# Layer 0 of a four-layer graph-attention stack: centring the norm by ScalarE's bias in place of a VectorE subtraction

## The chip, the cores and the metric

The kernel runs on one core of one Trainium2 chip. The metric is the device time of one execution in microseconds (us). Profiles are of one execution; their span goes from the first to the last instruction.

## The reference, cut to what matters

The input `x` is 8 batches x 2048 nodes x 64 features, and `adj` is a sparse 2048 x 2048 adjacency. Four layers follow one another. Each has the form `x = x + attention(relu(layernorm(x)), adj)`, where the norm is taken over the 64 features of each batch and node, without weights:

```python
def _layernorm(x, axis=-1, eps=1e-5):
    m = jnp.mean(x, axis=axis, keepdims=True)
    v = jnp.var(x, axis=axis, keepdims=True)
    return (x - m) / jnp.sqrt(v + eps)
```

Layer 0 is masked dot-product attention, softmax(h h^T / 8) h over the edges. Layer 1 is additive attention (GAT) with an ELU, layer 2 a four-head dot-product GAT with an output norm, layer 3 additive attention with a ReLU. What matters here is the norm that layer 1 takes of the `x` that layer 0 leaves: mean, variance, `(x - m) * rstd`, ReLU. The kernel computes it at the end of layer 0.

## The kernel before, in words

**Tiles.** All eight batches of a node lie in one row of 8 x 64 = 512 columns (`F`), so that a tile is 128 nodes x 512 columns, and there are 16 tiles (`NT`). The kernel works on edges, not on the dense matrix: each tile has lists of neighbours, a few of one neighbour per row (`ROWS`) and a few of packed edges (`PACKED`), and for each it gathers 128 rows of a table in HBM by an indirect DMA (`gather`, line 259). The table holds the normed `x` of all nodes (`store_rows`, line 363), with a row of column means as its last but one (lines 366 to 375: GpSimd sums the rows in `acc`, TensorE adds over the partitions, and a DMA writes the row). So the first gather of a layer needs all 16 tiles of the layer before.

**Stages.** `pipeline(*stages)` (line 218) goes over the tiles in a given order and runs stage s of tile n - s at step n, the oldest tile first. Two pipelines make up the time up to the end of layer 0. The first (line 710) loads `x`, norms it (`norm_a`, `norm_b`, `scaled`) and stores table 0. The second (line 711) has nine stages: load the adjacency tile; build the neighbour lists (`lists`, VectorE work for the most part); gather (`take0`); scores and exponentials (`first0`, with the load of the tile's `x`); row sums and the weighted sum of the gathered rows (`second`, whose products of rows and weights, line 389, run on GpSimd in layer 0, and whose sums run on TensorE); `third0`; `pre_b`; `pre_c`; `pre_d`. Layer 1 (line 719) ends in the same last stages.

**The norm.** `third0` divides by the row sums (line 480) and calls `add_store`: x is added (line 488), stored (line 489) and handed to `norm_a`. This has two forms. With `centre`, VectorE sums each batch (276), makes the mean in a small piece of a PSUM bank (`tiny`, 280) and subtracts it from the tile (283, into `ln_xc`), and ScalarE squares the centred tile in one instruction of 512 columns (284). Without `centre`, VectorE writes the negative mean to SBUF (`ln_m`, 288), and ScalarE squares x in eight instructions of 64 columns, one per batch, each with that batch's negative mean as bias (290). `norm_b` sums the squares (296), scales them (297), and GpSimd takes the power -1/2 (299); where the mean was not taken off, GpSimd also multiplies negative mean and rstd (301). `scaled` (307) applies rstd, and in the second form that product as bias, in eight ScalarE instructions of 64 columns together with the ReLU. Then TensorE transposes (315), ScalarE copies (316), two small products for layer 1's attention follow (354 to 357), and the rows are stored.

The first norm of layer 0, and the one after layer 1, take the form without `centre`; the norm after layer 0 and the two of layer 2 take the form with it.

**Buffers.** `x` tiles come from a pool of six buffers (line 498), `ln_xc` from one of three (282), `ln_m` from one of four. A buffer is free again when its last reader is done.

**What sets the order.** Every engine works through its own queue in order. The order in each queue is set when the program is built, by a list scheduler that simulates the engines and takes, of what is ready, what comes first in the program. So the order of the trace is not that of the source, and is fixed at run time: an instruction whose input is late holds all that stand behind it on its engine. Loads and stores issued by `nc.sync` stand in SP's queue, gathers in GpSimd's.

Of the kernel before, what the change touches and what calls it, by code (L numbers as in the profile page):

```python
# [61 lines left out]
def edge_stack(ctx: ExitStack, tc: tile.TileContext, x_in, adj, w1, w1t, a1, wh, wht, bh, wo, bo,  # L62
# [210 lines left out]
    def norm_a(src, st, centre):  # L273

        s = small.tile([P, B], F32, name="ln_s")
        nc.vector.tensor_reduce(s, heads(src), AX.X, OP.add)
        st["sq"] = rows_pool[0].tile([P, F], F32, name="ln_sq", bufs=4)
        if centre:
            mean = tiny(B)
            nc.vector.tensor_scalar(mean, s, INV_D, None, op0=OP.mult)  # L280
            st["less"] = None
            st["src"] = rows_pool[0].tile([P, F], F32, name="ln_xc", bufs=3)
            nc.vector.tensor_tensor(heads(st["src"]), heads(src), wide(mean), op=OP.subtract)
            nc.scalar.activation(st["sq"], st["src"], AF.Square)
            return
        st["src"] = src
        st["less"] = small.tile([P, B], F32, name="ln_m")
        nc.vector.tensor_scalar(st["less"], s, -INV_D, None, op0=OP.mult)
        for b in range(B):
            nc.scalar.activation(st["sq"][:, b * D:(b + 1) * D], src[:, b * D:(b + 1) * D], AF.Square,  # L290
                                 bias=st["less"][:, b:b + 1])
# [187 lines left out]
    def divide(st, dst):  # L479
        nc.vector.tensor_tensor(heads(dst), heads(st["y"]), wide(st["rec"]), op=OP.mult)  # L480

    def third0(i, st):
        divide(st, st["y"])
        add_store(i, st, st["y"], True)

    def add_store(i, st, p, centre, more=0.0):
        x = st["x"]
        nc.vector.scalar_tensor_tensor(x, p, more, x, op0=OP.add, op1=OP.add)
        nc.sync.dma_start(out=xs[i], in_=x)
        norm_a(x, st, centre)  # L490
# [98 lines left out]
    with tc.tile_pool(name="rows", bufs=2) as rp:  # L589
        rows_pool[0] = rp  # L590
        sel_all[0] = rp.tile([P, sum(PACKED) * P], F32, name="sel", bufs=1)
        with tc.tile_pool(name="lists", bufs=2) as pool, \
# [28 lines left out]
            def lists(i, st):  # L621
# [69 lines left out]
                for t0 in range(0, T, step):  # L691
# [7 lines left out]
                    for t in range(n):  # L699
# [9 lines left out]

            pipeline(xin_rows, lambda i, st: norm_a(st["x"], st, False), pre_b, pre_c(None), pre_d(0, None))  # L710
            pipeline(load_adj, lists, take0, both(first0, xin_rows), second, third0, pre_b, pre_c(u1),
                     pre_d(1, u1))

# [738 lines left out]
```

## Time and profile before

| | |
|---|---|
| Median of 3 runs | 1661.34 us (1655.29 to 1661.87) |
| The profiled execution | 1662.6 us, its span 1660.9 us |
| PE (TensorE matmul) busy | 1214.6 us, 73% |
| DVE (VectorE) busy | 1311.9 us, 79% |
| ACT (ScalarE) busy | 741.6 us, 45% |
| POOL (GpSimd) busy | 1151.1 us, 69% |
| First L488 of layer 0 (x added) | 153.5 us |
| Last scaling (L307) of layer 0 ends | 396.95 us |
| First gather of layer 1 starts | 404.64 us |
| Layer 0's stage, 150 to 390 us: DVE, POOL, PE, ACT busy | 232.0, 179.4, 168.3, 87.1 of 240 us |

A line of the trace names the source line (L283 is line 283), the engine, the operation, its output and inputs by the program's names, and their shapes. "POOL" is GpSimd, "PEld" TensorE's weight load, "SPq" SP's DMA queue; a "q" after an engine's name is its sequencer. In a timeline each row gives start, length, engine, line and operation; several equal instructions in a row are merged ("x8"), and in brackets stands how long the engine had been idle and what released it. In the view of a source line the three numbers are the minimum, median and maximum length in ns of one instruction.

### The profile page before, as it was taken

To read this page: it belongs to the slowest core of one execution; us is meant where nothing else is said; L and a number is where in the kernel's file an instruction comes from. 1 tells how busy PE (TensorE), PEld (TensorE's weight loads), DVE (VectorE), ACT (ScalarE), POOL (GpSimd) and SP (SyncE) were. 2 spreads that over 40 slices of the span, in tenths; PEclk is the share of its full clock that TensorE was granted. 3 is DMA by queue.
4 is the path that set the end of the run, shared out by engine and by line. 5 is a ranking of instruction groups with operands and counts; after the bars stand their busy time and mean duration, and the time that the engine had idled before them with its cause. 6 is when DMAs were issued, how large, how long until landed. Compare 5 with 4: busy or idle time off the path is not lost. (4 is left out here: it accounts for less than half of the span.)

```text
span 1660.9 us, 15702 instructions
## 1 busy us (share of the span) xinstructions
PE 1214.6 (73%) x3771; PEld 606.7 (37%) x3771; DVE 1311.9 (79%) x2674; ACT 741.6 (45%) x2362; POOL 1151.1 (69%) x903
## 2 busy tenths in 40 slices
PE   0025576776789974599997999999576868846898
PEld 0012243343454541234343344443233424423555
DVE  5978999994669987799999799861179979954667
ACT  5851223443257783356632455554334445560011
POOL 5765866786764215899689889998277889656650
PEclk9998877986889997799999999999877978857899
DMA  5545554453776537656255345300273443126771
GB/s 167 181 163 179 171 191 164 140 193 125 213 256 231 183 157 271 233 180 222 92 202 184 123 142 188 138 13 13 102 259 121 146 127 114 64 77 198 228 213 63
DMA packets 85787, 266.94 MB, mean 161 GB/s; under 512 B 14627, under 2 KB 14659, under 8 KB 75446
## 3 DMA queue, kind: packets, MB, share of 16 engines
q0 software_dynamic: 37328, 141.05, 27.4%
q1 hardware_dynamic: 48358, 124.79, 21.0%
q8 instruction: 32, 0.52, 0.1%
q14 instruction: 69, 0.57, 0.1%
HBM read 208.74 MB, written 57.05 MB: 160 GB/s over the span
## 5 line engine op out<-in xcount | busy, mean ns | idle before, releaser
L259 POOL DMA_INDIRECT g<-table,idx x405 | 396.2, 978 | 222.4 <-issue 131.7
L782 POOL TENSOR_TENSOR wh<-g,w 128x1024 f32<-128x1024 f32 x162 | 307.3, 1917 | 30.0 <-PE y L797 27.9
L394 PE MATMUL y<-wg,ident 128*128 128x512 f32 x392 | 232.4, 720 | 74.4 <-POOL wg L389 67.8
L299 POOL TENSOR_TENSOR ln_r<-ln_q,mhalf 128x8 f32<-128x8 f32 x80 | 135.9, 1702 | 129.0 <-DVE ln_q L297 93.0
L769 DVE TENSOR_REDUCE s<-prod 128x32 f32<-128x2048 f32 x81 | 183.9, 2285 | 14.6 <-ACT w L771 14.4
L389 POOL TENSOR_TENSOR wg<-g,w 128x1024 f32<-128x1024 f32 (+1 forms) x91 | 160.0, 1767 | 39.7 <-ACT w L445 31.7
L797 PE MATMUL y<-wh,ident 128*128 128x512 f32 x320 | 154.3, 609 | 28.1 <-POOL wh L795 24.4
L394 PE MATMUL y<-wg,selt 128*128 128x512 f32 x256 | 142.7, 669 | 6.0 <-POOL wg L389 6.0
L394 PEld LDWEIGHTS y<-wg,ident 128*128 128x128 f32 x392 | 79.6, 223 | 160.4 <-POOL wg L389 82.8
L797 PE MATMUL y<-wh,selt 128*128 128x512 f32 x256 | 124.6, 613 | 10.4 <-POOL wh L782 10.4
L805 ACT ACTIVATE yn<-y,rec 128x64 f32<-128x64 f32 x512 | 110.7, 366 | 27.6 <-PE y L797 26.8
L765 DVE TENSOR_TENSOR prod<-q,g 128x2048 f32<-128x2048 f32 x49 | 111.4, 2274 | 5.2 <-ACT g L763 5.1
L389 DVE TENSOR_TENSOR wg<-g,tiny 128x1024 f32<-128x1024 f32 (+1 forms) x92 | 98.1, 1086 | 12.3 <-PE y L394 11.9
L451 DVE SCALAR_TENSOR_TENSOR zt<-m,bhc,att 128x512 f32<-128x512 f32 x64 | 47.2, 737 | 74.9 <-ACT att L450 74.8
L408 PE MATMUL m<-w,selt 128*128 128x8 f32 (+1 forms) x384 | 61.0, 262 | 54.0 <-ACT w L554 19.1
L408 PEld LDWEIGHTS m<-w,selt 128*128 128x128 f32 x384 | 63.7, 215 | 100.0 <-ACT w L554 26.6
L307 ACT ACTIVATE xh<-x,ln_r 128x64 f32<-128x64 f32 x256 | 88.2, 427 | 25.5 <-POOL ln_r L301 25.4
L797 PEld LDWEIGHTS y<-wh,ident 128*128 128x128 f32 x320 | 58.9, 193 | 104.1 <-issue 64.4
L763 ACT COPY g<-g 128x512 f32<-128x512 f32 x81 | 50.4, 622 | 98.6 <-DVE prod L765 92.6
L437 PE MATMUL q<-rows,sel 128*128 128x512 f32 x128 | 81.4, 739 | 15.4 <-DVE prod L431 8.0
L765 DVE TENSOR_TENSOR prod<-qe,g 128x2048 f32<-128x2048 f32 x32 | 73.0, 2281 | 15.6 <-DMA qe<-qtab,qidx 14.5
L315 PE MATMUL q<-ident,xh 128*128 128x128 f32 x192 | 51.3, 341 | 44.9 <-ACT xh L307 43.1
(208 smaller groups left out, 2593.9 us busy)
## 6 DMA issues: line engine op xcount, KB each, us to landing
qtab<-q SPq DMA_DIRECT2D x16, 1040.0 KB, 4.0
a<-in_adj_dram SPq DMA_DIRECT2D x16, 1024.0 KB, 7.2
q<-qtab SPq DMA_DIRECT2D x14, 1040.0 KB, 5.3
table<-xh SPq DMA_DIRECT2D x48, 256.0 KB, 2.0
rows<-table SPq DMA_DIRECT2D x48, 256.0 KB, 3.8
xs<-x SPq DMA_DIRECT2D x48, 256.0 KB, 2.1
x<-xs SPq DMA_DIRECT2D x48, 256.0 KB, 3.6
table<-xh SPq DMA_DIRECT2D x32, 260.0 KB, 2.4
```

Source lines behind the costliest of these rows:

```text
L259: g = nc.gpsimd.indirect_dma_start(out=ring[:, (held[i] + t) % RING, :cols], out_offset=None, in_=table[k][:, :], in_offset=bass.IndirectO ...
L299: nc.gpsimd.tensor_tensor(st["rstd"][:, 0, :], q, mhalf, op=OP.pow)
L307: nc.scalar.activation(dst[:, b * D:(b + 1) * D], st["src"][:, b * D:(b + 1) * D], func, bias=0.0 if st["less"] is None else r[:, 1, b:b + ...
L389: eng.tensor_tensor(wg[:, :m].rearrange("p t (b d) -> p t b d", b=B), g[:, :, :F].rearrange("p t (b d) -> p t b d", b=B), w[:, t0:t0 + m, ...
L394: nc.tensor.matmul(y, lhs(i, t), wg[:, t - t0, :], start=(t == 0 and own is None), stop=(t == n - 1))
L408: nc.tensor.matmul(p[:, :cols], selt(i, t), packed[:, t, :], start=(t == 0), stop=(t == T - 1))
L437: nc.tensor.matmul(qe, sel(i, t - K), q, start=True, stop=True)
L765: nc.vector.tensor_tensor(pr.rearrange("p (b h) d -> p b h d", h=H), q[:, :B * H * D].rearrange("p (b h d) -> p b h d", h=H, d=D), heads(g ...
L769: nc.vector.tensor_reduce(s[:, t - lo, :], pr, AX.X, OP.add)
L782: nc.gpsimd.tensor_tensor(wg, heads(row(i, t))[:, :, None, :].to_broadcast([P, B, 2, D]), w[:, :, 2 * k:2 * k + 2, None].to_broadcast([P, ...
L797: nc.tensor.matmul(st["ys"][j], lhs(i, t), wg[:, 4 * j:4 * j + 4], start=False, stop=(t == n - 1))
L805: nc.scalar.activation(yn[:, b, h, :], st["ys"][j][:, b, h, :], AF.Copy, scale=st["rec"][:, 4 * j + b, 2 * k + h:2 * k + h + 1])
```

## The change

In `third0`, which only layer 0 uses, the norm is called without `centre`:

```diff
     def third0(i, st):
         divide(st, st["y"])
-        add_store(i, st, st["y"], True)
+        add_store(i, st, st["y"], False)
```

For each of the 16 tiles of layer 0 this has these effects in the program. On VectorE lines 280 (mean to PSUM) and 283 (subtraction, 128 x 512) fall away and line 288 (negative mean to SBUF, 128 x 8) comes in. On ScalarE one Square of 512 columns (284) becomes eight of 64 with a bias (290), and the eight scalings (307) read `x` and not `ln_xc`, and get a bias from SBUF in place of the constant 0. On GpSimd one product of 128 x 8 (301) is added. `ln_xc` isn't used in this layer, and `x` has a later last reader, line 307. No DMA is added, removed or changed. The result is the same up to rounding.

## Prediction

> **What bounds the kernel now.** First, the busy time of each engine by stretch. Columns: stretch, its length, then PE, PEld, DVE, ACT and POOL busy with instruction counts, the granted clock, the DMA share and GB/s.
>
> ```profile
> core 0: us, PE busy (x) PEld busy (x) DVE busy (x) ACT busy (x) POOL busy (x), PEclk, DMA share, GB/s
> 40.00:80.00 40.00, 0.00 (x0) 0.00 (x0) 38.25 (x155) 33.74 (x118) 26.39 (x23) 1.00 0.56 187
> 150.00:350.00 200.00, 135.84 (x418) 71.28 (x418) 193.69 (x577) 66.49 (x229) 143.57 (x105) 0.83 0.48 154
> 350.00:384.00 34.00, 28.87 (x120) 17.11 (x119) 33.24 (x90) 17.06 (x62) 31.77 (x24) 0.95 0.60 208
> 384.00:405.00 21.00, 14.28 (x45) 8.26 (x43) 6.63 (x15) 9.45 (x36) 9.14 (x8) 0.64 0.30 103
> ```
>
> The 16 changed steps lie between 153 us (first L488 of layer 0) and 397 us. Three limits follow one another. From 150 to 350 VectorE is busy 97% and ScalarE 33%: VectorE bounds. From 350 to 384 VectorE (98%) and GpSimd (93%) are both full. From 384 to 405 nothing is full: this is the drain of the last tiles, up to the first gather of layer 1, which needs every row of the table.
>
> Next, the instructions concerned, from the views of their source lines (ns min/median/max). The two of the 8-wide form run in layers 0 (first norm) and 1, with the code that the change switches to.
>
> ```profile
> L280 DVE TENSOR_SCALAR tiny<-ln_s x16: 143/155/170, 159.3 to 388.8; 128x8 f32<-128x8 f32 x16
> L283 DVE TENSOR_TENSOR ln_xc<-x,tiny x16: 625/675/687, 160.5 to 389.0; 128x512 f32<-128x512 f32 x16
> L284 ACT ACTIVATE ln_sq<-ln_xc x48: 613/629/643, 161.3 to 1487.4; 128x512 f32<-128x512 f32 x48
> L290 ACT ACTIVATE ln_sq<-x,ln_m x256: 331/333/351, 19.6 to 625.3; 128x64 f32<-128x64 f32 x128
> L307 ACT ACTIVATE xh<-x,ln_r x256: 423/425/444, 28.4 to 632.7; 128x64 f32<-128x64 f32 x128
> L307 ACT ACTIVATE xh<-ln_xc,ln_r x256: 331/333/361, 174.6 to 1492.8; 128x64 f32<-128x64 f32 x128
> L297 DVE TENSOR_SCALAR ln_q<-ln_q x15: 148/164/2566, 163.5 to 387.2; 128x8 f32<-128x8 f32 x15
> ```
>
> The maximum of L297 is to be seen: 2.57 us for eight columns. The timelines of VectorE and of GpSimd explain such cases; the clearest is L707:
>
> ```profile
> 176.60 3.93 DVE L707 TENSOR_SCALAR idx<-ke 128x2 int32<-128x2 f32 x1
> ```
> ```profile
> 176.19 1.89 POOL L389 TENSOR_TENSOR wg<-g,w 128x1024 f32<-128x1024 f32 x1
> 178.04 0.60 POOL L366 COPY acc<-xh 128x512 f32<-128x512 f32 x1
> 178.61 1.89 POOL L389 TENSOR_TENSOR wg<-g,w 128x1024 f32<-128x1024 f32 x1
> ```
>
> It ends at 180.53, and GpSimd's run of three instructions ends at 180.50. L297 at 201.64 ends at 204.21, an L389 of GpSimd at 204.16. So a small VectorE instruction that reads and writes SBUF is held until GpSimd is through. L280, which writes to PSUM, never exceeds 0.170.
>
> Last, the drain in the timeline:
>
> ```profile
> 387.12 3.81 ACT L307 ACTIVATE xh<-ln_xc,ln_r 128x64 f32<-128x64 f32 x15 [1.18 <-POOL ln_r L299]
> 391.56 0.62 ACT L284 ACTIVATE ln_sq<-ln_xc 128x512 f32<-128x512 f32 x1
> 394.93 2.02 ACT L307 ACTIVATE xh<-ln_xc,ln_r 128x64 f32<-128x64 f32 x8 [0.66 <-POOL ln_r L299]
> ```
> ```profile
> 404.64 1.04 POOL L259 DMA_INDIRECT g<-table,idx  x1 [6.29 <-DMA table<-mr]
> ```
>
> ScalarE works in order: the last tile's Square (input ready at 389.71) starts at 391.56, behind the scaling of the tiles ahead of it.
>
> [...] the trace has 333 and 425, and eight in a row take 2.02 us (pitch 0.241) and 2.76 us (pitch 0.333, at 486.20)[...]. L283 has one input in PSUM, and its spread of 625 to 687 shows no hold.
>
> **The change part by part**, per tile, 16 tiles.
>
> VectorE loses L283. What it frees is the time to the next start: 345.87 to 346.47, so 0.60 us, 9.6 in all. The group's busy time of 10.7 is the other bound.
>
> VectorE loses L280 and gets L288. Unheld they cost the same (0.155; L288 0.162 median in layer 1). But L288 writes SBUF, so it can be held. Layer 1 doesn't show it (maximum 0.172 there), since GpSimd makes no weighted products in it. The like instructions from 150 to 390 do: L297, L652, L654, L707 and L708 sum to 6.7+6.9+6.0+8.6+2.9 = 31.1 us for 60, mean 0.518, which is 0.36 over the 0.16 of an unheld one. Cross-check: L389 fills 76.6 of these 240 us; an arrival at random meets it in 32% of cases and waits half of 1.88, 0.30, and some more for L368. I take 0.36 (16 tiles: 5.8); the bounds are 0 (all as in layer 1) and 0.53 (all as L652).
>
> ScalarE: one Square of 0.54 pitch (0.63 less the overlap) becomes eight in 1.92 (8 x 0.241), and eight scalings of 1.93 become 2.66 (8 x 0.333): 2.1 us more, 34 in all, so 87.1 of 240 us becomes 121, 50%. This lies beside VectorE's work, and costs only where VectorE waits for ScalarE. Its waits now: L412 for L445 2.3, L296 for the Square 0.7. In proportion to the load these grow by 1.2; I take +1. Bounds: 0, and +4. In the 40 us from 40 to 80, with these very 8-wide forms, ScalarE is busy 84% and VectorE still 96%. If the cover goes, each tile pays up to a burst: the slower rival below. Queued behind a burst on ScalarE are L678 (for L679), L428 (for L431), L445 (for GpSimd's L389) and L685.
>
> GpSimd gets L301, 0.202 us in layer 1, 3.2 us in all; hidden until 350 (143.6 of 200 us busy), on the path for the three tiles from 350 to 384: +0.6. Bounds 0 and 3.2.
>
> DMA: nothing is issued, removed or moved. But the scaling now reads x itself, so x's buffer is held from L283 until the scaling, two stages longer, and the next x load behind it on SP's queue is issued later. The pool has six buffers, and the load that goes out at 161.24, after the first L283, serves a tile six ahead, some 90 us later at 15 us per tile. The first scaling ends at 176.7. Cost nothing; if that cover is gone, one landing, 2.9 us.
>
> The drain. Call the last three tiles A, B, C, on the clock of before, with GpSimd's last product ending at 384.06. Square(A) starts at 382.7 (its L288 is held behind one L389), Square(B) at 384.7 to 386.7. Reduction, L297, power (1.65) and L301 (0.2) follow: A is ready at 387.5, B at 389.5. Scaling A 387.5 to 390.2. L480 of C, behind B's reduction, starts at 387.4 instead of 386.65, so C's Square is ready at 389.6. If it goes ahead of scaling B, 390.2 to 392.1, C's power ends at 394.9 and its scaling at 397.8: +0.8 against 396.95. If it goes behind B and B's copy, 393.4 to 395.4, C's scaling ends at 401.0: +4.1. Before has the latter order, so I take +4.1, and keep 0.8.
>
> **Sum.** The first 11 L283s lie before 350 us; the other five lie where GpSimd's block or the drain sets the end, so only 11 count: -11 x 0.60 = -6.6; holds 11 x 0.36 = +4.0; waits for ScalarE +1.0; GpSimd +0.6; drain +4.1. Together +3.1 us. Against the profiled execution (1662.6: span 1660.9 and 1.7 around it) that is 1665.7. That execution is 1.3 over the median of the runs, 1661.3, so the forecast is **1664**. After 405 us everything is only shifted.
>
> **The rivals.** Half a percent, 8.3 us, is about what a measurement of this kernel can tell from no change.
>
> Faster: VectorE's cut passes in full. L288 falls between GpSimd's products, GpSimd's block starts and moves earlier, and C's Square slips ahead: -9.6 + 0.8 = -8.8, about 1652.5. For it: VectorE is full from 150 to 390. Against it: 31 us of held small instructions in that stage, and GpSimd's own 93% from 350.
>
> Slower: ScalarE's bursts stop VectorE. One mechanism: an instruction that VectorE needs, L678 for the selection matrix or L428 for the queries, stands behind a burst of 1.9 or 2.7 us, and VectorE, in order, waits with L679 or L431. One such wait per tile of half a burst, 1.15, in all 16 tiles is 18.4; in half of them 9.2. With +2.1 from the rest, about 1673 to 1682. It decides from (8.3 - 2.1) / 16 = 0.4 us per tile. For it: VectorE's waits for ScalarE are small only because ScalarE is 36% busy. Against it: 40 to 80 us.
>
> That the change does nothing on the chip is ruled out: its lines differ.
>
> **How the numbers follow.** Forecast within half a percent: 0.58. Faster rival: 0.16. Slower rival: 0.22. The forecast's dear corner (holds at 0.53, waits +4) with a drain that is worse than drawn: 0.04, slower. So faster 0.16, same 0.58, slower 0.26. The likeliest case's own range is 1655 (holds 0, drain +0.8, waits 0: -6.6 + 0.6 + 0.8 = -5.2) to 1669 (-6.6 + 5.8 + 4 + 0.6 + 4.1 = +7.9). For 8 in 10 it reaches into both rivals: **1652 to 1673**.
>
> **What would show it.** L283 in layer 0 gone from VectorE and 256 more short activations: certain. L288 between 150 and 400: a mean near 0.5 and single ones over 1 us confirm the hold; all under 0.2 refute it. VectorE's waits for L678, L428 and Square under 5 us in sum confirm the cover; 10 or more mean the slower rival. The first gather of layer 1 at 408 (404.64 + 3.1) tells the sum; the time from GpSimd's last product of layer 0 to that gather, 20.6 now, should be some 24. I am wrong if that gather comes before 398 or after 412, or if later layers change in length by more than a few us.

## The result, and the profile after

| | before | after |
|---|---|---|
| Median of 4 runs | 1661.2 us (1655.29 to 1661.87) | 1701.68 us (1697.76 to 1709.05) |
| The profiled execution, its span | 1662.6, 1660.9 us | 1699.15, 1697.4 us |

The ratio is 1.0248 [1.0224, 1.0273]: the kernel is 2.5% slower, where the prediction had 1664 us and at most 1673. Before any line of detail, the span is cut at the starts of six instructions that both traces have: the first sum of the changed norm (first L276 of `third0`), the first gather of layer 1, the last store of layer 1's query table (L345), the last L846 product of layer 2, the DMA of the row of means ahead of layer 3's gathers (last L375), the last output (L917). All are in us; only the second column holds changed code.

| | up to first sum | sum to gather | layer 1 | layer 2 | up to the mean row | rest |
|---|---|---|---|---|---|---|
| before | 156.1 | 248.5 | 241.8 | 541.7 | 311.6 | 156.6 |
| after | 154.3 | 255.2 | 257.5 | 543.5 | 320.5 | 161.8 |
| difference | -1.8 | +6.6 | +15.7 | +1.8 | +8.9 | +5.2 |

Of the 36.3 us, 31.5 lie in layers 1 to 3, whose source is the same to the letter. How far one profile can be trusted is shown by a second one of before (e9 below): the same stretch of the same program differs in it by up to 3 us.

First the changed part. The view of the engines' busy time by stretch, of the kernel after (the last stretch ends at its first gather):

```profile
40.00:80.00 40.00, 0.00 (x0) 0.00 (x0) 37.71 (x152) 33.46 (x117) 26.39 (x22) 1.00 0.54 182
150.00:350.00 200.00, 138.14 (x422) 72.96 (x420) 190.33 (x580) 89.22 (x312) 148.85 (x120) 0.78 0.51 159
350.00:384.00 34.00, 26.62 (x97) 15.33 (x97) 29.89 (x68) 18.49 (x67) 26.93 (x21) 0.90 0.45 154
384.00:409.00 25.00, 16.81 (x58) 10.08 (x56) 7.93 (x17) 16.13 (x59) 11.38 (x11) 0.66 0.35 119
```

VectorE (the third busy column) falls from 193.7 to 190.3 and from 33.2 to 29.9 us, and ScalarE (the fourth) rises from 66.5 to 89.2 in the long stretch. VectorE is no longer full from 350 to 384. The source-line view of the new step, for all three norms that have it:

```profile
L288 DVE TENSOR_SCALAR ln_m<-ln_s x48: 147/170/1903, 18.1 to 641.4; 128x8 f32<-128x8 f32 x48
```

The maximum of 1903 ns shows the hold; the 16 of layer 0 average 0.53 us (16 rows of VectorE's timeline, added up). The longest runs from 315.02 to 316.92, an L389 of GpSimd from 315.00 to 316.90. The drain, in ScalarE's and GpSimd's timelines:

```profile
390.09 2.76 ACT L307 ACTIVATE xh<-x,ln_r 128x64 f32<-128x64 f32 x8 [0.94 <-POOL ln_r L301]
392.75 2.00 ACT L290 ACTIVATE ln_sq<-x,ln_m 128x64 f32<-128x64 f32 x8
394.66 0.76 ACT L307 ACTIVATE xh<-x,ln_r 128x64 f32<-128x64 f32 x2
```
```profile
409.44 1.04 POOL L259 DMA_INDIRECT g<-table,idx  x1 [7.38 <-issue]
```

The last tile's Squares stand between the scalings of two tiles, and the gather starts 4.8 us later than before.

Now the unchanged part. One wait of VectorE and the longest of GpSimd from 420 us to 680 us, which is layer 1 and the start of layer 2, as the view of waits gives them (total, times, longest), before and then after:

```profile
DVE ln_q L296 <- ACT ln_sq L290: 4.3, 3, 2.0
POOL ln_r L299 <- DVE ln_q L297: 35.4, 5, 8.9
```
```profile
DVE ln_q L296 <- ACT ln_sq L290: 12.3, 8, 2.2
POOL ln_r L299 <- DVE ln_q L297: 71.3, 9, 14.2
```

VectorE waits for the Squares 8 times in place of 3, in a layer that had the eight Squares all along. A likely reason is in the queues, where an instruction that waits stops what stands behind it. In layer 0 of the kernel after, VectorE is idle for 3.15 us until the adjacency load for L626 has landed; L433, the next in its queue, reads what L431 had written by 213.00, and starts at 218.71:

```profile
212.32 0.68 DVE L431 TENSOR_TENSOR prod<-q,g 128x512 f32<-128x512 f32 x1
216.50 2.29 DVE L626 SCALAR_TENSOR_TENSOR a<-a,keyrow 128x2048 f32<-128x2048 int32 x1 [3.15 <-DMA a<-in_adj_dram]
218.71 0.68 DVE L433 TENSOR_REDUCE s<-prod 128x8 f32<-128x512 f32 x1
```

When the rows of both traces are laid side by side, 153 of the 368 rows that VectorE has in layer 1 stand in the same sequence, 178 of the 493 between layer 2 and the row of means, and 769 of ScalarE's 831 in layer 2; behind the row of means all rows of VectorE, ScalarE and GpSimd do. So the list scheduler, which orders all queues when the program is built, dealt other orders to most of what comes behind the change, and the last +5.2 us need another reason.

### The profile page after: what moved, and what is told of

Same layout as the page of the kernel before. It is cut to its first block, busy times and chain, and to the rows that moved or that the text cites. A ratio compares the mean times of both kernels' runs of the same rounds, so it can differ in the third digit from the quotient of the medians.

```text
span 1697.4 us, 15806 instructions
## 1 busy us (share of the span) xinstructions
PE 1227.2 (72%) x3771; PEld 613.8 (36%) x3771; DVE 1316.9 (78%) x2658; ACT 772.5 (46%) x2474; POOL 1156.3 (68%) x919
## 5 line engine op out<-in xcount | busy, mean ns | idle before, releaser
L782 POOL TENSOR_TENSOR wh<-g,w 128x1024 f32<-128x1024 f32 x162 | 307.1, 1917 | 29.6 <-PE y L797 27.5
L299 POOL TENSOR_TENSOR ln_r<-ln_q,mhalf 128x8 f32<-128x8 f32 x80 | 135.7, 1699 | 161.5 <-DVE ln_q L297 138.1
L389 POOL TENSOR_TENSOR wg<-g,w 128x1024 f32<-128x1024 f32 (+1 forms) x91 | 160.3, 1772 | 33.8 <-ACT w L445 17.3
L307 ACT ACTIVATE xh<-x,ln_r 128x64 f32<-128x64 f32 x384 | 133.3, 428 | 42.1 <-POOL ln_r L301 39.3
L805 ACT ACTIVATE yn<-y,rec 128x64 f32<-128x64 f32 x512 | 110.8, 366 | 30.9 <-PE y L797 30.2
L389 DVE TENSOR_TENSOR wg<-g,tiny 128x1024 f32<-128x1024 f32 (+1 forms) x92 | 98.3, 1088 | 18.0 <-PE y L394 17.6
L290 ACT ACTIVATE ln_sq<-x,ln_m 128x64 f32<-128x64 f32 x384 | 96.2, 335 | 34.0 <-DVE ln_m L288 34.0
L437 PE MATMUL q<-rows,sel 128*128 128x512 f32 x128 | 82.7, 747 | 14.8 <-DVE prod L439 9.9
L368 POOL TENSOR_TENSOR acc<-acc,xh 128x512 f32<-128x512 f32 x45 | 61.8, 1373 | 37.0 <-ACT xh L307 36.1
```

Source lines behind the costliest of these rows:

```text
L299: nc.gpsimd.tensor_tensor(st["rstd"][:, 0, :], q, mhalf, op=OP.pow)
L307: nc.scalar.activation(dst[:, b * D:(b + 1) * D], st["src"][:, b * D:(b + 1) * D], func, bias=0.0 if st["less"] is None else r[:, 1, b:b + ...
L389: eng.tensor_tensor(wg[:, :m].rearrange("p t (b d) -> p t b d", b=B), g[:, :, :F].rearrange("p t (b d) -> p t b d", b=B), w[:, t0:t0 + m, ...
L782: nc.gpsimd.tensor_tensor(wg, heads(row(i, t))[:, :, None, :].to_broadcast([P, B, 2, D]), w[:, :, 2 * k:2 * k + 2, None].to_broadcast([P, ...
L805: nc.scalar.activation(yn[:, b, h, :], st["ys"][j][:, b, h, :], AF.Copy, scale=st["rec"][:, 4 * j + b, 2 * k + h:2 * k + h + 1])
```

## Experiments

**Theories.** "Order": layers 1 to 3 are slower because their queues hold another order. Rival "state": they are slower because layer 0 leaves the engines or DMA queues otherwise at run time. For what layer 0 costs there are four: holds of VectorE, ScalarE's bursts, the longer hold of `x`, and layer 0's own order.

**How an order is held.** The built program of one kernel gives, per engine, the sequence of its instructions. This edit adds, in the other kernel, an ordering dependence without a semaphore between each instruction and the next of that list, so that it adds no wait at run time:

```diff
-            order[:] = ORDER1
+            order[:] = ORDER1; mark = len(nc.cur_bb.bb.instructions)
...
+        pin(tc, nc.cur_bb.bb.instructions[mark:])
...
+            if last is not None:
+                tc.add_manual_dep(traced[at], traced[last].name, mybir.DependencyInfo(
+                    mybir.DependencyClass.NoSync, mybir.DependencyReason.DATA), reason="order")
```

From `mark` on it holds layers 1 to 3; without `mark`, layer 0 too. That the hold does this can be read from the traces: in e1 and e10 all rows of VectorE and ScalarE in layers 1 to 3 stand as in before, and in e2 as in the kernel after. That it costs nothing is shown by e17 and e18 (1.0011 and 0.9996), which are held throughout.

The runs were made in five sets. In two of these before itself takes 1705 to 1708 us (e5 to e8; e17 and e18), in the others 1662 to 1664. So ratios are against before in the same set, and stretches are compared among like sets. The last two columns are from the profiled execution, which is one run and can lie some us beside the median.

| run | ratio | sum to gather | layers 1 to 3 |
|---|---|---|---|
| before; again (e9) | 1; 1.0008 [0.9991, 1.0025] | 248.5; 246.7 | 1251.7; 1254.5 |
| after | 1.0248 [1.0224, 1.0273] | 255.2 | 1283.3 |
| e1, change, later order of before | 1.0110 [1.0085, 1.0135] | 254.3 | 1256.5 |
| e10, the same again | 1.0097 [1.0079, 1.0115] | 257.3 | 1251.4 |
| e2, before, later order of change | 1.0166 [1.0138, 1.0193] | 247.0 | 1277.5 |
| e3, change, 8 buffers for x | 1.0119 [1.0085, 1.0154] | 263.9 | 1258.6 |
| e4, before, 7 buffers | 1.0154 [1.0124, 1.0184] | 255.4 | 1271.3 |
| e11, Squares alone, later order held | 1.0108 [1.0088, 1.0128] | 261.5 | 1251.7 |
| e12, biased scaling alone, later order held | 1.0113 [1.0093, 1.0133] | 262.9 | 1258.0 |
| e13, change, 8 buffers, later order held | 1.0063 [1.0043, 1.0082] | 260.2 | 1254.1 |
| e14, change, mean on ScalarE, later order held | 1.0054 [1.0036, 1.0071] | 261.3 | 1250.9 |
| e15, both | 1.0067 [1.0041, 1.0092] | 258.6 | 1252.8 |
| e16, before, 7 buffers, later order held | 1.0081 [1.0061, 1.0102] | 256.2 | 1256.5 |
| e17, before, 7 buffers, all held | 1.0011 [0.9994, 1.0028] | 246.6 | 1296.8 |
| e18, the same but SyncE in layer 0 | 0.9996 [0.9982, 1.0011] | 248.6 | 1301.8 |
| e5, change, all held but SyncE in layer 0 | 1.0089 [1.0068, 1.0111] | 260.5 | 1296.7 |
| e6, the same, mean on ScalarE | 1.0089 [1.0068, 1.0110] | 258.6 | 1302.5 |
| e7, change, 7 buffers | 1.0225 [1.0194, 1.0256] | 262.2 | 1321.4 |
| e8, biased scaling alone | 1.0244 [1.0218, 1.0269] | 262.0 | 1322.7 |

### e1 and e2: the orders of layers 1 to 3 exchanged

e1 is the change with layers 1 to 3 held in the sequences of before, e2 is before with those of the change.

> The changed layer 0, with the instructions of layers 1 to 3 held, on each engine, in the order in which they stand in the kernel before. Theory 'order': of the 36.5 us that the changed kernel's profile shows more, only the 4.8 up to the first gather of layer 1 belong to the changed instructions, and 31.7 to the other order in which the scheduler dealt the unchanged later layers. So about 1661 + 5 = 1666 us (1662 to 1670), and the first gather of layer 1 at about 409. Rival 'state': what layer 0 leaves behind at run time (x buffers freed later, a later start of loads, the granted clock) slows the later layers, whatever their order. So about 1695 to 1702.

> The kernel before, with the instructions of layers 1 to 3 held, on each engine, in the order in which they stand in the changed kernel. Theory 'order': 1661 + 32 = 1693 us (1688 to 1698), with the first gather of layer 1 still at about 405. Rival 'state': about 1661 to 1665.

Measured: 1681.15 us (1675.16 to 1682.5) and 1689.99 us (1686.98 to 1693.52), before there 1663.6. e2 met the number of the order theory. e1 missed both: layers 1 to 3 are back to 1256.5 us, but 1.1% stays. The state theory, which had e1 at 1695 to 1702 and e2 at 1661 to 1665, falls. That the order makes the later layers slower is shown from both sides: before, with not one instruction changed, takes 1277.5 us for them with the other order, 23 to 26 us more than in its own two profiles, and has the same waits in layer 1 as the kernel after. In e2:

```profile
DVE ln_q L296 <- ACT ln_sq L290: 13.1, 8, 2.2
POOL ln_r L299 <- DVE ln_q L297: 71.0, 9, 14.2
```

and in e1 they are near those of before:

```profile
DVE ln_q L296 <- ACT ln_sq L290: 6.3, 4, 2.0
POOL ln_r L299 <- DVE ln_q L297: 27.7, 4, 8.9
```

The same in the busy time by stretch, 500 to 600 us, which lies in layer 1: before, after, e2, e1 in this sequence.

```profile
500.00:600.00 100.00, 92.53 (x341) 48.65 (x339) 95.82 (x187) 77.81 (x214) 30.32 (x32) 0.98 0.54 193
```
```profile
500.00:600.00 100.00, 85.97 (x305) 45.11 (x305) 86.52 (x166) 67.06 (x185) 27.26 (x29) 0.96 0.53 188
```
```profile
500.00:600.00 100.00, 84.29 (x305) 43.95 (x304) 85.19 (x161) 68.93 (x194) 23.97 (x26) 0.98 0.50 177
```
```profile
500.00:600.00 100.00, 94.36 (x351) 49.31 (x349) 95.31 (x190) 73.83 (x201) 30.75 (x33) 1.00 0.60 211
```

VectorE is 96 and 95% busy with the order of before, 87 and 85% with that of the change, whichever work layer 0 has done.

### e3, e4 and e7: only the number of x buffers

e3 and e7 are the change with 8 and 7 buffers for `x`, e4 is before with 7:

```diff
-            load(st, "x", src(i), 6)
+            load(st, "x", src(i), 7)
```

> The change with eight buffers for x in place of six. Here the scheduler's order of layer 1 comes out all but that of before (370 of 372 rows of VectorE the same), that of the layer 2 and 3 norms in between (338 of 493). Theory 'order': layer 1 as long as before (257 us from its first gather to the first load of layer 2's queries, where the changed kernel has 273), part of the rest given back, so 1668 to 1685. Rival 'buffers' (x held two stages longer makes loads late): also layer 1 as before, but then it is the loads, which the waits for x would show. If neither: 1700.

> The kernel before with seven buffers for x: no instruction is added or removed, but the scheduler deals the order of all layers anew (229 of 372 rows of VectorE the same in layer 1, 210 of 493 in the part after layer 2). Theory 'order': the order of before is better than what the scheduler usually deals, so this is slower too, by 10 to 40 us (1670 to 1700). Rival 'state': no change, 1657 to 1665.

> The change with seven buffers for x. The scheduler's order of layer 2 comes out as in the kernel before, that of the part after it nearly so (464 of 493 rows of VectorE), that of layer 1 new. Theory 'order': the part after layer 2 as long as before (some 312 us from the end of layer 2 to the mean row, where the change has 320), layer 1 as it falls (242 to 258 us), so 1667 to 1690. Rival 'state': as the change, 1695 to 1702.

Measured: 1681.23 (1678.32 to 1687.88), 1687.3 (1684.29 to 1689.14) and 1743.77 us (1739.16 to 1749.41; before there 1705.16). e4 does the same work as before with a buffer more, and is 1.5% slower: its layer 1 takes 248.1 and its part up to the mean row 318.2 us. The change is 1.2% slower than before with 8 buffers and 2.25% with 7: buffers act here as a new deal of the queues. No single one of these can be read as the price of a buffer. e3 and e4 fell into the ranges of the order theory. e7 did not: 1667 to 1690 us against a before of 1661 is a ratio of 1.003 to 1.017, and its layer 1, dealt anew, took 277.5 us, where before with every queue held takes 259.0 in such a set (e17).

### e5 and e6: all queues held

e5 is the change with every common instruction of every layer in the sequence of before, except SyncE's in layer 0; L288 stands where L280 stood, the eight Squares where the one did, and L301 behind L299. e6 also makes layer 0's negative mean on ScalarE, so that nothing small is left on VectorE to be held:

```diff
-        nc.vector.tensor_scalar(st["less"], s, -INV_D, None, op0=OP.mult)
+        nc.scalar.activation(st["less"], s, AF.Copy, scale=-INV_D) if early[0] else nc.vector.tensor_scalar(st["less"], s, -INV_D, None, op0=OP.mult)
```

> The change, with every instruction that it shares with the kernel before held in the order of before on VectorE, ScalarE, GpSimd and TensorE in all layers (and on SP from layer 1 on); line 288 stands where 280 stood, the eight Squares where the one stood, 301 behind its 299. What is left is the changed instructions alone. Theory 'order': the time of these is what the prediction's sum gave, near +3 us, with ScalarE's longer steps meeting an order made for short ones (+0 to +7), so 1664 to 1672. Rival 'the change itself': the +17 of the run before, whose layer 0 the scheduler had dealt, is the price of the instructions, so 1676 to 1684.

> As the run with all pinned, but the negative mean of layer 0 (128 x 8) is made by ScalarE, directly ahead of its Squares, and not by VectorE's line 288, which GpSimd can hold. Theory 'hold': line 288 took 0.525 us in the mean in the change, 0.36 over an unheld one, so VectorE's stage is shorter by up to 16 x 0.45 = 7 us, of which some 11 of 16 tiles count: 4 to 5 us less than the run with all pinned. Rival: the hold is hidden, no difference (within 2 us).

Measured: 1720.67 (1715.77 to 1722.68) and 1721.38 us (1715.86 to 1726.83), before there 1705.16: 0.9% each, some 15 us. My theory (0 to 7 us) missed, and the rival (15 to 23 us) holds: in before's own order the change's work costs 15 us. e6 shows that taking L288's holds off VectorE doesn't help: 16 x 0.48 us leave it, for 16 short instructions more on ScalarE, and nothing is gained.

### e8: half of the change, order free

The subtraction and the one Square stay; only the scaling reads `x` with a bias (`i0` is set in layer 0 alone):

```diff
-            st["less"] = None
+            st["less"] = None if i0[0] is None else small.tile([P, B], F32, name="ln_m")
...
-            nc.scalar.activation(st["sq"], st["src"], AF.Square)
+            nc.scalar.activation(st["sq"], st["src"], AF.Square); i0[0] is None or (nc.vector.tensor_scalar(st["less"], s, -INV_D, None, op0=OP.mult), st.__setitem__("src", src))
```

> Half of the change: VectorE still subtracts the mean and ScalarE squares the centred tile in one instruction, but the scaling reads x with a bias, so that 288 and 301 come in and x is held longer. The order from layer 2 on comes out exactly as in the change, that of layer 1 is a third one. Theory 'order': from layer 2's end on as long as in the change and in the run of before with the order of the change (320 us to the mean row), and slower in all by 10 to 40 us: 1672 to 1700. Rival 'Squares' (the eight short Squares on ScalarE make the loss): little loss here, 1662 to 1670.

Measured: 1747.65 us (1744.37 to 1748.86), 2.4%. From layer 2 on it has the very order of the change, and costs as much, without having taken anything off VectorE or added a Square. The rival, which made the Squares the loss, falls; the order theory's range (up to 1.023) was just passed.

### e9 to e12: a profile of before on the same chip, and the halves with the later order held

e9 is before again, e10 is e1 again. e11 has the eight Squares with bias, and VectorE still makes a centred tile for the scaling, by adding the negative mean (on line 291, `less` is the tile of line 287); e12 is e8 with layers 1 to 3 held.

```diff
-                                 bias=st["less"][:, b:b + 1])
+                                 bias=less[:, b:b + 1]); i0[0] is None or b or (st.__setitem__("src", rows_pool[0].tile([P, F], F32, name="ln_xc", bufs=3)), nc.vector.tensor_tensor(heads(st["src"]), heads(src), wide(less), op=OP.add), st.__setitem__("less", None)) 
```

> The kernel before, unchanged, for its layer lengths on the chip of this run: layer 0, layer 1, the rest. Every theory expects a ratio of 1.000 within 0.003. Against the first profile of it (layer 0 404.6 us, layer 1 241.9, layer 2 541.7, to the mean row 311.6, rest 156.6) each stretch within 1 us if the chip is as fast; all longer by like shares if it is slower.

> The change, with layers 1 to 3 in the queue order of before, once more, beside a profile of before on this chip. It ran 1.1% slower than before when first measured, of which its profile showed 7.5 us in layer 0 and some 5 us in the layers behind. If the remainder is the cost of layer 0 itself (a layer that runs 12 to 18 us longer in the median run than before's), its profile shows layer 0 longer by 12 to 18 us and layers 1 to 3 within 2 us together. If the remainder lies in later layers, which the order doesn't explain, layer 0 is longer by 4 to 8 us and the layers behind by 6 to 12. Ratio 1.008 to 1.013 by both.

> Half of the change alone, layers 1 to 3 in the queue order of before: the eight Squares with a bias replace the one Square in layer 0, and the scaling stays as it was, from a tile that VectorE centres (with the negative mean added), so VectorE saves nothing. Layer 0 has 112 more instructions on ScalarE, no product more on GpSimd. If the Squares cost what remains (ScalarE later, and VectorE and GpSimd behind it), the ratio is 1.007 to 1.013; if it is the lasting hold of x and the bias of the scaling, it is 1.000 to 1.004.

> The other half alone, layers 1 to 3 in the queue order of before: the subtraction and the one Square stay, and the scaling reads x with a bias, so x is held until the scaling and GpSimd makes one product of 256 elements more for a tile. VectorE saves nothing and makes the negative mean besides (16 x some 0.2 to 0.5 us). If the longer hold of x and GpSimd's product cost what remains, the ratio is 1.007 to 1.013; if the Squares do, it is 1.001 to 1.005 (the negative mean and its holds alone).

Measured: 1665.38 (1657.76 to 1667.22), 1678.08 (1674.1 to 1681.53), 1680.58 (1675.91 to 1683.98) and 1683.35 us (1675.74 to 1686.34), before there 1661.9. Layers 1 to 3 of all four profiles lie within 4 us of 1254.5, so what is left lies for the most part between first sum and first gather: +10.6, +14.8 and +16.2 us. Each half costs as much as the whole, and the rivals of e11 and e12 both came true: the cost isn't a sum of two parts. But neither half takes anything off VectorE, and both give it more: up to its last L296 it is busy 234.6 (e11) and 237.9 us (e12), against 226.8 in e9. That is half and more of what they lose. The source-line views, of e12 and e11:

```profile
L284 DVE TENSOR_SCALAR ln_m<-ln_s x16: 153/160/5106, 160.2 to 403.2; 128x8 f32<-128x8 f32 x16
```
```profile
L291 DVE TENSOR_TENSOR ln_xc<-x,ln_m x16: 674/683/5962, 161.2 to 402.7; 128x512 f32<-128x512 f32 x16
```

The negative mean averages 1.02 us in e12 (16.4 us for 16), and the addition 1.09 in e11, where L283 in before, with the mean in PSUM, takes 0.67 and at most 0.69.

### e13 to e16: what frees layer 0, and the control

e13 has 8 buffers for `x`, e14 the negative mean on ScalarE, e15 both, each in the change with layers 1 to 3 held. e16 is e4 (before with 7 buffers) with layers 1 to 3 held. The edits are those shown above.

> The change with 8 buffers for x, layers 1 to 3 in the queue order of before. If loads of x that wait for a buffer (14.7 us of SyncE's queue, 5 times, in the change with this order) make VectorE late, layer 0 is 5 to 10 us shorter than in the change with the order alone (415.8 us) and the ratio falls from 1.010 to 1.003 to 1.006. If not, it stays at 1.008 to 1.012.

> The change with layer 0's negative mean made on ScalarE instead of VectorE (so that it holds VectorE no more), layers 1 to 3 in the queue order of before. The hold theory: 8.6 us of VectorE go, layer 0 ends near 409 and the ratio is 1.004 to 1.006. If waits set the length of layer 0 and not VectorE's work, the time that is saved turns into waits and the ratio stays at 1.008 to 1.012.

> Both: 8 buffers for x and the negative mean on ScalarE, layers 1 to 3 in the queue order of before. If holds of VectorE and loads of x share what is lost, the ratio is 0.998 to 1.003; if ScalarE's chain of Squares and scalings causes the waits, it stays at 1.008 to 1.012.

> The kernel before with 7 buffers for x and no other change, layers 1 to 3 in the queue order of before. Without that order it was 1.5% slower. The order theory: layers 1 to 3 are as before, and the ratio is 0.998 to 1.004, whatever layer 0's new order does in 2 or 3 us. If the buffers themselves cost 1.5%, it stays at 1.012 to 1.018.

Measured: 1673.69 (1669.91 to 1677.06), 1672.22 (1668.82 to 1677.0), 1672.4 (1667.27 to 1679.63) and 1675.75 us (1671.82 to 1679.83), before there 1662.19. The first three lie 0.3 to 0.4% under e10, together no lower than alone. Of what was expected of them only e14's ratio came true, and its layer 0, which should have ended near 409 us, ended at 419.4. The profiles can't tell where the 0.3% comes from: e10's is of its fastest run (1674.1 us, median 1678.08), e14's of its slowest, so that all four profiled runs took 1672 to 1677 us. What they do show is that time taken off VectorE turned into waits. In e14 and e15 it is busy only 216.2 and 216.7 us up to its last L296, against 225.2 in e10 and 226.8 in e9, and the stretch is no shorter: it waits 20.3 and 12.3 us for TensorE, in e10 3.2.

e16 met neither range: with no work changed and the later order held it is 0.8% slower. From first sum to gather it takes 8 to 9 us more, but its first sum comes 4 to 7 us earlier than in before's two profiles, so that the gather itself is only 2 to 4 us late; 6 us lie behind the row of means. It left one explanation to try, layer 0's own order.

### e17 and e18: the control with layer 0 held too

Both are before with 7 buffers; e17 holds every queue of every layer, e18 all but SyncE's in layer 0, as e5 did.

> Before with 7 buffers for x, every queue of every layer in the old order, so that only the place and the number of buffers differ. If the order of layer 0 is what cost 0.8%, the ratio is 0.998 to 1.003. If the buffers themselves (their places, what the seventh lets start) cost it, it stays at 1.006 to 1.010.

> The same, but SyncE's queue in layer 0 is left to be dealt anew, as it was in the change with all orders held. If SyncE's order alone costs what that one kept, the ratio is 1.006 to 1.010; if it doesn't matter, 0.998 to 1.003, and then what the change kept with all orders held is the work of the change itself.

Measured: 1708.76 (1704.19 to 1716.19) and 1707.31 us (1699.3 to 1712.79), before there 1707.83. So the buffer costs nothing, and SyncE's order doesn't matter. What e16 has and e17 has not is the new order of layer 0, so this is where its 0.8% comes from, though the two ran in different sets. It also makes e5 readable: held as e18, with the change's work, 0.9% is the work's own price in that order. e5 and e17 ran in two sets that agree (layers 1 to 3 take 1296.7 and 1296.8 us, the gather comes at 415.9 and 404.0), and their waits of VectorE from 150 to 405 us say where it goes. The longer ones for ScalarE, and the one for TensorE that grew most, of e17, then e5:

```profile
DVE ln_q L296 <- ACT ln_sq L284: 3.0, 2, 2.4
DVE row L412 <- ACT w L445: 2.3, 2, 2.1
DVE rec L474 <- PE m L408: 0.7, 1, 0.7
```
```profile
DVE ln_q L296 <- ACT ln_sq L290: 12.4, 10, 5.6
DVE row L412 <- ACT w L445: 3.7, 2, 3.2
DVE rec L474 <- PE m L408: 2.8, 1, 2.8
DVE prod L431 <- ACT q L428: 2.2, 1, 2.2
```

From the first L276 to the end of the last L296, e17 takes 235.0 us (VectorE busy 226.5, idle 8.5) and e5 247.7 (217.5, 30.2): 9.0 us of work less, 21.8 of waiting more. Of that 14.0 are for ScalarE (5.3 and 19.3), 9.4 of these for the Squares; 5.8 are for TensorE. The longest wait, in e5's timelines of VectorE and of ScalarE:

```profile
396.65 0.17 DVE L541 COPY tiny<-f1s 128x8 f32<-128x8 f32 x1
402.46 0.69 DVE L296 TENSOR_REDUCE ln_q<-ln_sq 128x8 f32<-128x512 f32 x1 [5.64 <-ACT ln_sq L290]
```
```profile
394.63 5.08 ACT L307 ACTIVATE xh<-x,ln_r 128x64 f32<-128x64 f32 x15 [0.94 <-POOL ln_r L301]
399.61 0.56 ACT L316 COPY xt<-q 128x512 f32<-128x512 f32 x1
400.07 0.44 ACT L307 ACTIVATE xh<-x,ln_r 128x64 f32<-128x64 f32 x1
400.42 2.01 ACT L290 ACTIVATE ln_sq<-x,ln_m 128x64 f32<-128x64 f32 x8
```

The negative mean is ready at 396.7, the Squares start at 400.4 behind sixteen scalings at a pitch of 0.333, and VectorE stands for 5.6 us. No run took ScalarE's bursts away alone, so that these waits set the length is read from the trace and not tried.

## Why the prediction was wrong, step by step

**"After 405 us everything is only shifted": this step failed.** It carried no term, and 31.5 of the 36.3 us of the profile lie there. With the later order of before the same change takes 1251.4 to 1256.5 us for layers 1 to 3, where before takes 1251.7 and 1254.5; with the later order of the change, before takes 1277.5. In ratios: the order costs 1.4 to 1.5% with the change's work (1.0248 against 1.0110 and 1.0097) and 1.7% with before's. The list scheduler was described ahead of the prediction, as the thing that orders every queue; that a changed instruction in layer 0 can make it deal later layers anew was not thought through. My own check, "if later layers change in length by more than a few us", named the right symptom.

**The sum up to the gather was too small as well.** Forecast +3.1, and +4.8 in the profile after, which looks near. But nearly the same layer 0 reaches the gather at 412.1 us in e1 and 415.8 in e10, 6 to 11 us later than before's two profiles (404.6 and 406.1), and with the later order held the change costs 1.0 to 1.1%. On before's 1661.2 us that is 1677 to 1679, past the 1673 that the prediction allowed: without the new later order it would have missed too. That +4.8 came so near was in part luck. Its terms:

- *VectorE: right.* Forecast -6.6 + 4.0 = -2.6 for 11 tiles, or by the same prices -9.6 + 5.8 = -3.8 for 16. Busy up to the last L296: 226.6 and 226.8 before, 223.0 after, -3.6 to -3.8 (in e10, 225.2). The instruction with its hold, 0.52 forecast, was 0.53. The five L288 that start while GpSimd is in an L389 or an L368 take 0.55 to 1.90 us and end within 0.05 us of it; the other eleven take 0.15 to 0.18. Not every small instruction is held: an L707 at 300.43, inside an L389 that ends at 300.73, takes 0.14. What makes the hold was not shown.
- *"Waits for ScalarE +1.0", and nothing for any other wait: mis-sized.* VectorE's idle time in that stretch grew from 10.3 and 8.2 to 18.2 us, 8 to 10 more. Added up by what ended them, its waits for ScalarE grew from 5.3 to 8.2, those for the adjacency load (L626) from 1.7 and 0 to 6.2, those for TensorE from 2 to 3.3. In before's own order, e5, the ScalarE part alone grew by 14.0. Scaling up waits by ScalarE's load was the wrong rule: what a burst costs depends on where it stands in the queue. The slower rival had the mechanism and, for e5, the size (9.2 to 18.4), though most of these waits were for the Squares and not for L678.
- *ScalarE's work itself* was as the trace of before has it for these forms in other norms (0.333 and 0.425 us): the Squares with a bias (L290) take 0.333 us, the scalings with one (L307) 0.426, and in a row of eight they start 0.241 and 0.333 apart. From first sum to gather it is busy 122.1 us, 31 more than before, where 34 were forecast. The "256 more short activations" were miscounted: 128 short Squares are new, and 128 scalings that were there already get a bias.
- *Drain.* From GpSimd's last product to the gather forecast some 24 us, measured 23.4 (before 20.6). The Squares of the last tile slipped ahead of a scaling, the branch that I priced at +0.8. That the number fits is luck: the 2.8 us have other parts, among them a gather that starts 7.4 us after the last sum of `acc`, in before 6.3.
- *DMA, "cost nothing".* Not settled. Loads of `x` do wait for ScalarE's scaling now (in e10 14.7 us of SyncE's queue, in e9 none). With 8 buffers in a newly dealt order they wait 46.6 us (e13), VectorE's wait for the adjacency load is only 1.3, and the gather still comes at 414.0, between those of e1 and e10. Whether the held `x` makes the adjacency load late was not tried.
- *The range.* Its low end is off by one: 1661.3 - 5.2 is 1656.

**What the change itself is worth.** In before's sequence its work costs 0.9% (e5): by the trace, ScalarE's longer bursts stop VectorE. In the scheduler's own sequence for layer 0 it costs 1.0 to 1.1% (e1, e10), and the later order that comes with it another 1.4 to 1.5%. The time of before rests on its order: with no work changed, another order in layer 0, behind it or in both makes it 0.8 to 1.7% slower (e16, e2, e4).

**What stays open.** In e16 and e12 the stretch behind the mean row takes 162.8 and 161.2 us in place of 156.6, with every queue there in the old order; in the kernel after, where that part has the old order too, 161.8. Order doesn't explain these 5 to 6 us. Nor does a profile show why e13 to e15 are 0.3% faster than e10. No version beat before.

## What to carry to other kernels

Where a list scheduler orders the queues, an edit in one layer can be a new deal for the layers behind it, and that can cost more than the edit is about (here 1.5 of 2.5%): cut both spans at the same events first, and if layers that the diff doesn't touch change their length, hold the order before asking what the edit does. A change of a pool size with no work in it is a cheap control for this. And on an in-order engine at half load, price a longer burst by what stands right behind it, not by the engine's load: here, in one order, VectorE waited 3 us more for ScalarE (after), in another 14 (e5).

## What the runs showed that was not expected

- A 512-column VectorE instruction can run far over its median too: the addition in e11 with both inputs in SBUF averaged 1.09 us (median 0.68) and once took 5.96, the like subtraction in before with its mean in PSUM 0.67 and at most 0.69. The form with the small operand in PSUM was 0.4 us shorter for a tile here; that GpSimd held the other was not shown.
- Taking 10 us of work off VectorE (e14, e15: busy 216 and 217 us in place of e9's 227) left a stage, in which it had been 97% busy, no shorter.
- The same program takes 259 us for layer 1 and 181 us behind the mean row in some sets (e17), and 241 and 157 in others (e9), while layer 0, layer 2 and the part between agree within 3 us. The record gives e13 to e16 (before at 1662 us) and e17 and e18 (1708) the same chip number, 3, so the chip alone doesn't account for it. What differs is a few long stalls for which the view of waits finds no releaser among the engines' instructions (it says "remote"). In all six profiles of the two slower sets ScalarE stands 26 to 27.5 us before one L579 of layer 1; the other fourteen profiles have no such wait over 4 us after the first 150 us. From e17's waits, 404 to 470 us:

```profile
ACT e L579 <- remote: 27.5, 1, 27.5
```

From 436 to 448 us of this stall TensorE does nothing and VectorE 0.35 us of work, while GpSimd goes on gathering. What they wait for was not found.
